# Attention 1 of a graph network: features in two halves, the table in four parts, counts and dense blocks started two blocks earlier

## The chip, the cores and the metric

The kernel runs on one core of a Trainium2 chip. The core has five instruction streams: TensorE (PE, with its weight loads shown as PEld), VectorE (DVE), ScalarE (ACT), GpSimd (POOL) and SyncE (SP, which here only starts transfers). Each engine works through its own list in order; semaphores tie the lists together. The metric is the device time of one execution in microseconds (us), as the median of several runs; lower is better.

## The reference

A pre-norm residual block is applied twice to 6250 nodes of 128 features. The first application is a two-layer graph attention over 200000 edges sorted by destination, the second a graph convolution over the same edges. Cut to what matters here:

```
h  = relu(layernorm(x))
feat = h @ W1;  el = sum(feat*al1);  er = sum(feat*ar1)       # 4 heads of 16
e  = leaky_relu(el[src] + er[dst]);  alpha = softmax of e over the edges of each dst
g  = elu(segment_sum(feat[src] * alpha, dst) + b1)             # attention 1
g2 = the same with W2, one head of 128                         # attention 2
x  = x + g2
x  = x + convolution(relu(layernorm(x)), src, dst, edge attributes)
```

## The kernel before, in words

Nodes are cut into 49 blocks of 128 (`NB`). The program has three large stages: attention 1, attention 2 and the convolution. Only the features and attention 1 are touched by the change.

**Features.** `norm_coefs` computes mean and variance of all 49 blocks on VectorE (`bn_stats`, `bn_aggr`), then one square root on ScalarE, a reciprocal and a bias. Then a loop takes four blocks at a time: ScalarE normalizes (`h`), TensorE transposes, VectorE copies the transposes, TensorE multiplies by the extended weights, ScalarE copies the result into `t1` (64 features and 4 source scores), VectorE copies the destination scores into `er1`. After the loop, two exponentials of the clipped scores complete the 76 columns of `t1`, and one transfer on SP's queue writes `table1` to DRAM (1862 KB). `pq`, `pq3` and `sel1` (factors of the destination side and a steep offset for the dense blocks) come from the same data.

**Attention 1** treats its destination blocks in two ways. The first 31 (`NG = NB - DENSE1`) are attended by gathering. For each block, 34 columns of 128 edges are handled in five groups of 8, 8, 8, 8 and 2 (`GROUPS`, `K = 34`). A group is 8 indirect transfers on GpSimd's queue (`gather`, line 315, table rows into one of six `G` buffers), then `attend`: a one-hot tile, a small product, weights and messages on VectorE, a split into two parts (`halve`: ScalarE casts, VectorE subtracts), and eight accumulating products (line 377). Line 967 is ScalarE's copy that closes a block; every fourth block is finished by `finish1`.

The last 18 blocks (`DENSE1`) are attended densely, two at a time, from a matrix of edge counts: 7 ramps on ScalarE (line 870), a minimum on VectorE (872) and products with the right-hand side `rhs1` (890). `n_dense` = 270 steps cover all of it, 252 of them with 7 ramps each. The count matrices of all 49 blocks are needed (attention 2 reads them as well). They are built in 196 quarter-block steps (`count`: two one-hot tiles on VectorE at line 752, 16 products on TensorE, 4 casts `ca` on ScalarE at 765, one transfer to DRAM), beginning with block 30.

**Order of the work.** The Python loop over the 31 gathered blocks decides what is emitted beside each group. Side work comes first: window searches (`seek_windows`, 25 indirect transfers `wpart_i` on GpSimd and two VectorE operations each), the copies of the edge lists that overlap (`write_runs`, transfers on ScalarE's queue), and `fill_rhs1` (seven fills in blocks 1 and 2). From block `LAG` on, `due` hands out count steps in proportion to the gathers, and from block `LAG_D` on dense steps. `fetch_run` gathers the edge lists of a window on GpSimd (line 710), and `cut_windows` turns them into keys on VectorE (from line 719). A dense pair loads the counts of its blocks on SP's queue, so those must have been written. Within what is emitted, a scheduler of the framework sorts the instructions of each engine ahead of time by its own estimates, so the order in the trace is not quite that of the source. On the engines the order is then fixed.

```python
            if b < LAG - 1:
                for _ in range(2):
                    next(seeking, None)
            if b + 1 < LAG:
                write_runs(b * len(GROUPS) + q, (LAG - 1) * len(GROUPS))
            ...
            due = len(steps) * ((b - LAG) * K + s + n) // ((NG - LAG) * K)
            ...
            due = n_dense * ((b - LAG_D) * K + s + n) // ((NG - LAG_D) * K)
```

Of the kernel before, what the change touches and what calls it, by code (L numbers as in the profile page):

```python
# [30 lines left out]
F32 = mybir.dt.float32  # L31
# [4 lines left out]
AF = mybir.ActivationFunctionType  # L36
OP = mybir.AluOpType
# [5 lines left out]
P = 128  # L43
# [7 lines left out]
WSTEP = 16  # L51
HS = 7
CT, LT = 30, 40
LAG = 5
AHEAD = 4
DENSE1, LAG_D = 18, 7
GP, GK, GSB = 125, 16, 4
SEG = 40
FAR = 1.0e30
# [1 line left out]
SPREAD = 60.0  # L61
SLOPE = 0.2
# [4 lines left out]
def gnn_kernel(ctx: ExitStack, tc: tile.TileContext, x, src, dst, attr4, attr8,  # L67
               W1, al1, ar1, b1, W2, al2, ar2, b2,
               Wl0, Wl1, Ws0, Ws1, Wm1, Wm2, Wtp, Wf0, Wf1, src_t, dst_t, attr4_t, attr8_t, out):
    nc = tc.nc  # L70
    N, D = x.shape
    E = src.shape[0]
    NB = -(-N // P)
    FULL = N // P
    REST = N - FULL * P
    HD = W1.shape[1]
    H1, DH = al1.shape
# [22 lines left out]
    work = ctx.enter_context(tc.tile_pool(name="work", bufs=2))  # L100
# [9 lines left out]
    def small():  # L110
        return ps_sm.tile([P, 512], F32, tag="small", name="small")
# [4 lines left out]
    def bank():  # L116
        return ps_bank.tile([P, 512], F32, tag="small" if ps_bank is ps_sm else "bank", name="bank")
# [40 lines left out]
    pool = one.enter_context(tc.tile_pool(name="att1", bufs=1))  # L158
# [3 lines left out]
    pre = seek.enter_context(tc.tile_pool(name="pre1", bufs=1))  # L162
    xt = pre.tile([P, NB, D], F32, name="xt0")
# [94 lines left out]
    def write_runs(i, n):  # L258

        per = ROWT // WSTEP  # L260
        j, i, n = i * 2 // n, i % (n // 2), n // 2
        ends = [(GP - 1) * i // n, (GP - 1) * (i + 1) // n]
        for p0, p1, m in [(*ends, per)] + [(GP - 1, GP, NROW - (GP - 1) * per)] * (i == n - 1):
            a = raws[j][p0:p1, :]
            nc.scalar.dma_start(
                runs[p0 * per:p0 * per + (p1 - p0) * m, j, :].rearrange("(p r) t -> p r t", r=m),
                bass.AP(tensor=a.tensor, offset=a.offset, ap=[a.ap[0], [WSTEP, m], [1, WCAP]]))
# [18 lines left out]
        nc.vector.tensor_scalar(dstw[:, b, :], raw_dst.pop(b), -float(b * P), None, op0=OP.add)  # L286


    def norm_coefs(pool, b0=0, n=NB):

        mv = pool.tile([P, n, 2], F32, name=f"mv{n}")
        for j in range(n):
            st = work.tile([P, 6], F32, name="bnst")
            nc.vector.bn_stats(st, xt[:, b0 + j, :])
            nc.vector.bn_aggr(mv[:, j, :], st)
        sd = pool.tile([P, n], F32, name=f"sd{n}")
        nc.scalar.activation(sd, mv[:, :, 1], AF.Sqrt, bias=eps)
        scale = pool.tile([P, n], F32, name=f"scale{n}")
        nc.vector.reciprocal(scale, sd)
        bias = pool.tile([P, n], F32, name=f"bias{n}")  # L300
        nc.vector.scalar_tensor_tensor(bias, mv[:, :, 0], -1.0, scale, op0=OP.mult, op1=OP.mult)
        return scale, bias

    def transposed(srcs, rows, evict):

        ps = bank().rearrange("p (j c) -> p j c", j=4)
        for j, s in enumerate(srcs):
            nc.tensor.transpose(ps[:rows, j, :], s, ident)
        t = work.tile([P, 4, P], F32, name="transp")
        evict(t[:rows, :len(srcs), :], ps[:rows, :len(srcs), :])  # L310
        return t
# [30 lines left out]
    def load_low(b):  # L342
        t = aw.tile([P, CAP], BF16, name="oht")
        nc.sync.dma_start(t, dlow[ds(window_start(b), CAP)].partition_broadcast(P))
        return t
# [173 lines left out]
    def rows_of(table, b0, n):  # L519
        return table[b0 * P:(b0 + n) * P, :].rearrange("(b p) f -> p b f", p=P)  # L520
# [20 lines left out]
    table1 = dram.tile([NB * P, R1], F32, name="table1")  # L541
# [21 lines left out]
    er1 = pool.tile([P, NB, H1], F32, name="er1")  # L563

    t1 = pre.tile([P, NB, R1], F32, name="t1")
    scale, bias = norm_coefs(pre)
    for b0 in range(0, NB, 4):
        bs = range(b0, min(b0 + 4, NB))
        hs = []
        for b in bs:  # L570
            h = work.tile([P, D], F32, name="h", bufs=4)
            nc.scalar.activation(h, xt[:, b, :], AF.Relu, bias=bias[:, b:b + 1], scale=scale[:, b:b + 1])
            hs.append(h)
        ht = transposed(hs, D, nc.vector.tensor_copy)
        ps = small()
        w = HD + 2 * H1
        for j in range(len(bs)):
            nc.tensor.matmul(ps[:, j * w:(j + 1) * w], ht[:, j, :], ext1, start=True, stop=True)
        ps = ps[:, :len(bs) * w].rearrange("p (b f) -> p b f", f=w)
        nc.scalar.copy(t1[:, b0:b0 + len(bs), :HD + H1], ps[:, :, :HD + H1])  # L580
        nc.vector.tensor_copy(er1[:, b0:b0 + len(bs), :], ps[:, :, HD + H1:])
    el = pre.tile([P, NB, H1], F32, name="el")
    nc.vector.tensor_scalar(el, t1[:, :, HD:HD + H1], SPREAD, -SPREAD, op0=OP.min, op1=OP.max)
    nc.scalar.activation(t1[:, :, HD + H1:HD + 2 * H1], el, AF.Exp)
    nc.scalar.activation(t1[:, :, HD + 2 * H1:], el, AF.Exp, scale=SLOPE)
    nc.sync.dma_start(rows_of(table1, 0, NB), t1)
    pq = pool.tile([P, NB, 2 * H1], F32, name="pq")
    node_factors(pq, er1, H1)
    split3(pre, pq3, pq, [P, NB, 2 * H1])
# [125 lines left out]
    def cut_windows(c):  # L715
        run = fetched.pop(c)
        si, di = run[:, 0, :], run[:, 1, :]
        hi = cut.tile([P, WCAP], I16, name="hi")
        nc.vector.tensor_scalar(hi, si, 7, None, op0=OP.logical_shift_right)
        key = cut.tile([P, WCAP], F32, name="key")  # L720
        far = cut.tile([P, WCAP], F32, name="far")
        nc.vector.tensor_scalar(key, di, own_w[:, c:c + 1], None, op0=OP.subtract)

        nc.vector.scalar_tensor_tensor(far, key, -1.0, key, op0=OP.add, op1=OP.mult)
        nc.vector.scalar_tensor_tensor(key, hi, float(W), key, op0=OP.mult, op1=OP.add)
        nc.vector.scalar_tensor_tensor(key, far, 1e4, key, op0=OP.mult, op1=OP.add)
        nc.vector.tensor_scalar(hi, si, P - 1, None, op0=OP.bitwise_and)
        lo = far
        nc.vector.tensor_copy(lo, hi)
        m = min(P, NSW - c * P)  # L730
        ps = quad()
        for j, v in enumerate((lo, key)):
            nc.tensor.transpose(ps[:, j, :m], v[:m, :], ident[:m, :m])
        t = cut.tile([P, 2, P], BF16, name="turned", bufs=2)
        nc.scalar.copy(t[:, :, :m], ps[:, :2, :m])
        return t
# [4 lines left out]
    written = set()  # L741
# [239 lines left out]
    for b in range(NG):  # L981
        if b == LAG - 1:
            deque(seeking, 0)
        if b == LAG:
            tables[chunks[0]] = cut_windows(chunks[0])
# [5 lines left out]
        for q, (s, n) in enumerate(GROUPS):  # L991
            step(attending(b, s, n, oht))
            if q == 2 and b + 1 < NG:
                low = load_low(b + 1)
# [5 lines that stand above are left out]
            if b == 1 or b == 2 and q < NB // HS - len(GROUPS):  # L1000
                fill_rhs1(((b - 1) * len(GROUPS) + q) * HS, HS)
            if b == LAG - 1 and q == 3:
                for c in chunks[:2]:
# [30 lines left out]
    xt = ctx.enter_context(tc.tile_pool(name="xt", bufs=1)).tile([P, NB, D], F32, name="xt")  # L1034
# [49 lines left out]
    with tc.tile_pool(name="att2", bufs=1) as pool, tc.tile_pool(name="dense", bufs=2) as dense, \  # L1084
# [8 lines left out]
        def finish2(b0, n):  # L1093
# [10 lines left out]
            nc.vector.tensor_add(xt[:, bs, :], xt[:, bs, :], ps[:, :n * D].rearrange("p (b f) -> p b f", f=D))  # L1104
            yield
            scale, bias = norm_coefs(fin, b0, n)
            t3 = fin.tile([P, 4, D], F32, name="t3")
            for j0 in range(0, n, 2):
# [35 lines left out]
        for b0 in range(0, NB, 2):  # L1144
            n = min(2, NB - b0)
# [10 lines left out]
            for h0 in range(0, NB, HS):  # L1156
# [3 lines left out]
                for h in range(HS):  # L1160
                    nc.scalar.activation(ramp[:, h, :n * P], pe[:, :n * P], AF.Relu,  # L1161
                                         bias=sel2[:, h0 + h, :], scale=STEEP)
                c = ct[:, :n, :, h0:h0 + HS, :].rearrange("p k a h d -> p h (k a) d")
# [12 lines left out]
            for k in range(n):  # L1176
                b = b0 + k
# [5 lines left out]
                                               op0=OP.mult, op1=OP.add)  # L1183
# [102 lines left out]
    with tc.tile_pool(name="conv", bufs=1) as pool, tc.tile_pool(name="gath3", bufs=6) as gath:  # L1286
# [43 lines left out]
        for t in range(0, NT, SB):  # L1330
            n = min(SB, NT - t)
# [8 lines left out]
            for j in range(2 if n > NPR else 1):  # L1340
                c = (t + j * NPR) * P
# [88 lines left out]
```

## Time and profile before

| quantity | value |
|---|---|
| median of 3 runs | 4651.73 us (4643.12 to 4654.26) |
| profiled execution | 4651.0 us, span of its instructions 4649.3 us |
| PE busy | 3221.1 us (69%) |
| DVE busy | 3499.3 us (75%) |
| ACT busy | 2828.8 us (61%) |
| POOL busy | 2785.6 us (60%) |
| first table gather | 133.6 us |
| first run gather | 427.3 us |
| closing copy of gathered block 31 | 1909.3 us |

Busy shares are over the whole span. Times in the trace count from its first instruction. A bracket behind a row says how long the engine was idle before it and what ended the idle time; "issue" is time in which it waited for nothing that the profile shows. ACTq and SPq rows are transfers issued on those engines' queues. A releaser is the last of several semaphores by the profile.

### The profile page before, as it was taken

What the parts mean: (1) busy time and instruction counts of PE and PEld (TensorE: products, weight loads), DVE (VectorE), ACT (ScalarE), POOL (GpSimd) and SP (SyncE); (2) the same over time, 40 slices, a digit from 0 to 9 for tenths busy, and PEclk for the clock granted to TensorE, in tenths of its full rate; (3) what the DMA queues carried; (4) which work ended last, traced back from release to release, by engine and by line L of the source; (5) the groups of instructions that cost most, each with busy time, mean ns of one, the idle gap of its engine ahead of it and who ended that gap; (6) DMA issues with size and microseconds to landing.
All of it is one profiled execution on the core that took longest, in us unless ns stands there. A gap on an engine that the chain in (4) does not pass through costs nothing. (4 is left out here: it accounts for less than half of the span.)

```text
span 4649.3 us, 65503 instructions
## 1 busy us (share of the span) xinstructions
PE 3221.1 (69%) x21547; PEld 2384.9 (51%) x21548; DVE 3499.3 (75%) x5685; ACT 2828.8 (61%) x6834; POOL 2785.6 (60%) x2684
## 2 busy tenths in 40 slices
PE   3023676766667766399997678777777777777777
PEld 3013566656566666388885344444444444444444
DVE  4255777878778878488886787788878777878787
ACT  2022578777878888499996554555555555555554
POOL 0677777666566665100002777777777777777774
PEclk9999766666666666599998676677677777766777
DMA  3344455555555555544442222222222222222221
GB/s 86 69 108 125 139 162 145 157 151 156 144 150 163 164 152 149 184 159 157 160 165 73 57 58 59 58 58 58 58 57 59 58 58 58 58 58 58 58 57 32
DMA packets 348162, 480.88 MB, mean 103 GB/s; under 512 B 190737, under 2 KB 236343, under 8 KB 343830
## 3 DMA queue, kind: packets, MB, share of 16 engines
q1 hardware_dynamic: 199542, 240.46, 16.9%
q0 software_dynamic: 85776, 147.31, 13.4%
q10 hardware_dynamic: 62480, 88.68, 5.6%
q8 instruction: 176, 2.88, 0.3%
q14 instruction: 188, 1.54, 0.1%
HBM read 367.21 MB, written 108.97 MB: 102 GB/s over the span
## 5 line engine op out<-in xcount | busy, mean ns | idle before, releaser
L315 POOL DMA_INDIRECT G<-table,srcc x1563 | 1592.8, 1019 | 1027.5 <-DVE kept L1210 551.4
L315 POOL DMA_INDIRECT G<-table,srcw x1054 | 1121.0, 1064 | 568.2 <-issue 279.0
L1262 PE MATMUL whole<-halves,ohr 128*128 128x512 f32 x1563 | 684.8, 596 | 362.2 <-DVE halves L332 320.1
L870 ACT ACTIVATE ramp<-erb,sel 128x256 bf16<-128x256 f32 x1764 | 759.0, 499 | 11.5 <-DVE up L872 8.0
L1262 PEld LDWEIGHTS whole<-halves,ohr 128*128 128x128 f32 x1563 | 427.5, 288 | 607.6 <-DVE halves L332 392.5
L1243 ACT ACTIVATE g<-G,a 128x128 f32<-128x128 f32 x1563 | 511.0, 395 | 43.5 <-DMA G<-table,srcc 35.0
L1161 ACT ACTIVATE ramp<-small,sel 128x256 bf16<-128x256 f32 (+1 forms) x1225 | 447.6, 625 | 61.1 <-DVE up L1165 26.1
L765 ACT CAST ca<-small 128x392 bf16<-128x392 f32 x784 | 342.1, 481 | 192.1 <-PE small L763 180.4
L890 PE MATMUL up<-rc,up 128*128 128x102 bf16 x3528 | 311.4, 264 | 155.9 <-DVE up L872 154.8
L377 PE MATMUL whole<-halves,ohr 128*128 128x136 f32 x1054 | 250.1, 387 | 224.6 <-DVE halves L332 167.7
L763 PE MATMUL small<-key,lo 128*128 128x98 bf16 x3136 | 318.6, 252 | 116.1 <-ACT ca L765 105.3
L1232 PEld LDWEIGHTS big<-wtp_sb,hid 64*128 64x128 f32 x3126 | 256.7, 239 | 204.7 <-ACT hid L1226 100.7
L890 PEld LDWEIGHTS <-up 128*128 128x128 bf16 x3528 | 265.7, 129 | 183.4 <-DVE up L872 177.4
L332 DVE TENSOR_TENSOR halves<-big,halves 128x1024 fp32r<-128x1024 f32 x196 | 237.4, 1211 | 144.3 <-ACT halves L331 144.3
L872 DVE TENSOR_TENSOR up<-ramp,ctc 128x1792 bf16<-128x1792 bf16 x252 | 273.9, 1087 | 92.7 <-ACT ramp L870 71.3
L1224 PE MATMUL small<-hid,wm_sb 128*128 128x512 f32 x392 | 288.0, 825 | 74.4 <-ACT hid L1222 74.2
L377 PEld LDWEIGHTS whole<-halves,ohr 128*128 128x128 f32 x1054 | 217.3, 292 | 237.1 <-DVE halves L332 172.4
L1232 PE MATMUL big<-wtp_sb,hid 64*128 64x128 f32 x3126 | 307.4, 344 | 26.8 <-ACT hid L1226 26.8
L763 PEld LDWEIGHTS <-lo 128*128 128x128 bf16 x3136 | 247.1, 124 | 145.1 <-issue 126.4
L752 DVE TENSOR_TENSOR lo<-slots,turned 128x2048 bf16<-128x2048 bf16 x196 | 239.0, 1219 | 101.4 <-PE small L763 100.2
L1222 ACT ACTIVATE hid<-small 128x512 f32<-128x512 f32 x196 | 116.8, 596 | 313.7 <-PE small L1220 313.7
L331 ACT CAST halves<-mid 128x1024 fp32r<-128x1024 f32 x196 | 204.1, 1041 | 160.9 <-DVE mid L1251 159.2
(292 smaller groups left out, 6196.7 us busy)
## 6 DMA issues: line engine op xcount, KB each, us to landing
counts<-ca ACTq DMA_DIRECT2D x196, 392.0 KB
ct<-counts SPq DMA_DIRECT2D x196, 392.0 KB
rc<-rhs SPq DMA_DIRECT2D x63, 717.5 KB
oht<-dlow SPq DMA_DIRECT2D x31, 1088.0 KB
ctc<-counts SPq DMA_DIRECT2D x504, 56.0 KB
G<-table,srcc POOLq DMA_INDIRECT x1563
G<-table,srcw POOLq DMA_INDIRECT x1054
a8t<-attr_rows SPq DMA_DIRECT2D x391, 16.0 KB
```

What stands on the lines that cost most here:

```text
L315: nc.gpsimd.indirect_dma_start(out=G[:, c, :], out_offset=None, in_=table, in_offset=bass.IndirectOffsetOnAxis(ap=idx[:, c:c + 1], axis=0))
L377: nc.tensor.matmul(acc, oh[:, c, :], ms[:, c].rearrange("e s f -> e (s f)"), start=start and c == 0, stop=stop and c == n - 1)
L763: nc.tensor.matmul(ps[:, k * NKEY:(k + 1) * NKEY], lo[:, a, :, r], ky[:, a, :, r], start=True, stop=True)
L765: nc.scalar.copy(ca[:, :, i * W:(i + WBANK) * W].rearrange("p h (k d) -> p h k d", d=W), ps[:, :WBANK * NKEY].rearrange("p (k h d) -> p h ...
L870: nc.scalar.activation(ramp[:, i, :n * P], erb[:, h, :n * P], AF.Relu, bias=sel1[:, h0 + i, h:h + 1], scale=STEEP)
L872: nc.vector.tensor_tensor(up[:, :, :n * P].rearrange("p h (a d) -> p h a d", d=QN), ramp[:, :, :n * P].rearrange("p h (a d) -> p h a d", d ...
L890: nc.tensor.matmul(ups[k][:, h], up[:, i, k * P:(k + 1) * P], by_head[:, i, :, h, :], start=h0 + i + h == 0, stop=h0 + i + h == NB + H1 - 2)
L1161: nc.scalar.activation(ramp[:, h, :n * P], pe[:, :n * P], AF.Relu, bias=sel2[:, h0 + h, :], scale=STEEP)
L1224: nc.tensor.matmul(ph[:, :npr * P], wm2_sb, hid1[:, :npr * P], start=True, stop=True)
L1232: nc.tensor.matmul(pw[:, c, :], hid2[half, j * P:(j + 1) * P], wtp_sb[half].rearrange("x p u -> x (p u)"), start=True, stop=True)
L1243: nc.scalar.activation(g0[:, c], G[:, c, :], AF.Copy, scale=a0[:, c, :])
L1262: nc.tensor.matmul(acc, oh[:, c, :], ms[:, c].rearrange("e s h i u -> e (s h i u)"), start=start, stop=stop)
```

## The change

Four edits, all up to the end of attention 1.

1. The statistics of the first 24 blocks (`H0`) are computed ahead of the loop; those of the other 25 are put into the first six turns of the loop, and their coefficients follow in the sixth.
2. The exponentials and the write of `table1` are done in parts of 12, 12, 12 and 13 blocks, the first two after the sixth turn, the others as soon as their blocks are there.
3. `LAG` goes from 5 to 3: counts begin at the gathered block of index 3, window searches are drained at the start of block 2, and `write_runs` cuts its work into 10 pieces over two blocks instead of 20 over four.
4. `LAG_D` goes from 7 to 5, so the dense steps begin at block 5.

The number of count steps and dense steps is the same; they are spread over 28 and 26 blocks instead of 26 and 24.

```diff
-LAG = 5
+LAG = 3
 AHEAD = 4
-DENSE1, LAG_D = 18, 7
+DENSE1, LAG_D = 18, 5
...
-    def norm_coefs(pool, b0=0, n=NB):
-
-        mv = pool.tile([P, n, 2], F32, name=f"mv{n}")
-        for j in range(n):
-            st = work.tile([P, 6], F32, name="bnst")
-            nc.vector.bn_stats(st, xt[:, b0 + j, :])
-            nc.vector.bn_aggr(mv[:, j, :], st)
+    def norm_stats(mv, b):
+        st = work.tile([P, 6], F32, name="bnst")
+        nc.vector.bn_stats(st, xt[:, b, :])
+        nc.vector.bn_aggr(mv, st)
+
+    def norm_coefs(pool, b0, n, mv=None):
+
+        if mv is None:
+            mv = pool.tile([P, n, 2], F32, name=f"mv{n}")
+            for j in range(n):
+                norm_stats(mv[:, j, :], b0 + j)
         sd = pool.tile([P, n], F32, name=f"sd{n}")
...
-    scale, bias = norm_coefs(pre)
+
+    H0 = NB // 8 * 4
+    mv = pre.tile([P, NB - H0, 2], F32, name="mv")
+    el = pre.tile([P, NB, H1], F32, name="el")
+    written = deque((H0 // 2 // 4 * 4, H0, (H0 + NB) // 8 * 4, NB))
+    b_out = 0
+    scale, bias = norm_coefs(pre, 0, H0)
+    co = [(scale[:, j:j + 1], bias[:, j:j + 1]) for j in range(H0)]
     for b0 in range(0, NB, 4):
...
-            nc.scalar.activation(h, xt[:, b, :], AF.Relu, bias=bias[:, b:b + 1], scale=scale[:, b:b + 1])
+            nc.scalar.activation(h, xt[:, b, :], AF.Relu, bias=co[b][1], scale=co[b][0])
             hs.append(h)
+        if b0 < H0:
+            for j in range((NB - H0) * b0 // H0, (NB - H0) * (b0 + 4) // H0):
+                norm_stats(mv[:, j, :], H0 + j)
+        if b0 + 4 == H0:
+            scale, bias = norm_coefs(pre, H0, NB - H0, mv)
+            co += [(scale[:, j:j + 1], bias[:, j:j + 1]) for j in range(NB - H0)]
         ht = transposed(hs, D, nc.vector.tensor_copy)
...
-    el = pre.tile([P, NB, H1], F32, name="el")
-    nc.vector.tensor_scalar(el, t1[:, :, HD:HD + H1], SPREAD, -SPREAD, op0=OP.min, op1=OP.max)
-    nc.scalar.activation(t1[:, :, HD + H1:HD + 2 * H1], el, AF.Exp)
-    nc.scalar.activation(t1[:, :, HD + 2 * H1:], el, AF.Exp, scale=SLOPE)
-    nc.sync.dma_start(rows_of(table1, 0, NB), t1)
+        while written and H0 <= b0 + 4 and written[0] <= b0 + len(bs):
+            c = slice(b_out, written.popleft())
+            nc.vector.tensor_scalar(el[:, c], t1[:, c, HD:HD + H1], SPREAD, -SPREAD, op0=OP.min, op1=OP.max)
+            nc.scalar.activation(t1[:, c, HD + H1:HD + 2 * H1], el[:, c], AF.Exp)
+            nc.scalar.activation(t1[:, c, HD + 2 * H1:], el[:, c], AF.Exp, scale=SLOPE)
+            nc.sync.dma_start(rows_of(table1, c.start, c.stop - c.start), t1[:, c])
+            b_out = c.stop
     pq = pool.tile([P, NB, 2 * H1], F32, name="pq")
```

## The prediction

> **What bounds the kernel now.** I read the stage windows first, because a busy share over 4649 us mixes three stages with different limits. Windows of the whole core (length; PE, PEld, DVE, ACT, POOL busy with instruction counts; granted TensorE clock; DMA share; GB/s):
>
> ```profile
> 133.00:395.00 262.00, 44.71 (x282) 40.77 (x281) 107.11 (x257) 38.17 (x54) 193.80 (x195) 1.00 0.42 101
> 682.00:1840.00 1158.00, 794.97 (x7667) 727.36 (x7667) 911.55 (x1622) 929.78 (x2306) 755.85 (x698) 0.66 0.53 154
> 1840.00:1915.00 75.00, 51.46 (x517) 46.43 (x515) 53.70 (x79) 66.76 (x166) 0.00 (x0) 0.64 0.33 108
> ```
>
> From 133 to 395 us GpSimd (POOL) alone is full: 195 gathers of 0.94 us with 0.3 us of issue after each, about 1.34 us apiece, while ScalarE is at 15% and VectorE at 41%. Counts and dense blocks have not begun. From 682 to 1840 us ScalarE is at 80%, VectorE at 79%, POOL at 65% (and 0.3 us of issue per gather on top). Past the last gather ScalarE rises to 89%. So one regime leaves ScalarE idle and the next leans on it. The same in the windows of the gather's line, L315 (gathers per stretch):
>
> ```profile
> 303.00:395.00 92.00, 70.07 (x69) 1.00 0.62 156
> 700.00:1840.00 1140.00, 723.97 (x668) 0.66 0.53 153
> ```
>
> 1.33 us per gather, or 45 us per block of 34, becomes 1.71 us, or 58 us.
>
> What lengthens a block? The timeline of ScalarE shows each block's closing copy (L967), and the windows of its ramp line, L870, show what was done in between:
>
> ```profile
> 1112.49 0.19 ACT L967 COPY sums<-whole 128x68 f32<-128x68 f32 x1
> 1152.42 0.21 ACT L967 COPY sums<-whole 128x68 f32<-128x68 f32 x1 [4.06 <-PE whole L377]
> 1231.22 0.19 ACT L967 COPY sums<-whole 128x68 f32<-128x68 f32 x1
> 1112.00:1152.00 40.00, 21.40 (x51) 0.66 0.59 175
> 1152.00:1231.00 79.00, 42.13 (x98) 0.66 0.48 137
> ```
>
> Two blocks, each of 34 gathers: 39.9 us with 51 ramps, 78.7 us with 98. Time goes with the counts and dense work, hardly with the gathers.
>
> Ahead of the gathers stands the feature stage. Timeline (start, length, engine, line, work, idle before and its end):
>
> ```profile
> 64.96 0.34 ACT L297 ACTIVATE sd<-mv,eps 128x49 f32<-128x49 f32 x1 [10.37 <-DVE mv L295]
> 66.07 3.96 ACT L572 ACTIVATE h<-xt,bias,scale 128x128 f32<-128x128 f32 x10 [0.78 <-DVE bias L301]
> 108.71 1.28 ACT L584 ACT_TABLE_LOAD   x1 [0.61 <-issue]
> 110.65 0.38 SPq L586 DMA_DIRECT2D table<-t  x1
> 133.60 0.96 POOL L315 DMA_INDIRECT G<-table,srcw  x1 [85.79 <-DMA table<-t]
> 427.28 0.94 POOL L710 DMA_INDIRECT run<-runs,wfirst  x1 [0.30 <-issue]
> 429.81 0.19 DVE L719 TENSOR_SCALAR hi<-run 128x128 int16<-128x128 int16 x1 [21.92 <-DMA run<-runs,wfirst]
> ```
>
> ScalarE waits for all 49 blocks' statistics, the loop runs 66.1 to 108.1 us, the table is issued at 110.65 and the first gather starts 22.9 us later. Counting begins with the first gather of runs at 427.3, and VectorE stood 21.9 us for it.
>
> **What the Trainium skill says.** "Perfetto Trace Analysis", Optimization Strategy: kernels with several regimes may gain by "interleaving those regimes". The windows show two such regimes. "DMA: Bandwidth & Descriptors", Issuing engines are not separate DMA queues: transfers started from any engine share the same 16 DMA engines. The table does land among the run writes of ScalarE's queue, with no gather yet running. "ScalarE: Activation LUTs", What ACT_TABLE_LOAD costs: about 1283 ns plus a drain; the trace has 1.28 us.
>
> **The change, part by part.** The scheduled order of both kernels was compared engine by engine. From attention 2 on, all that ScalarE, GpSimd and VectorE issue keeps its order, so I price nothing there; everything up to the end of attention 1 (1909 us, the last closing copy) moves.
>
> *Statistics in halves.* The 24th block's aggregate was already there at 50.4 us; a mask operation (1.02 us), the reciprocal and the bias follow, so h starts near 52.5 instead of 66.1: 13.6 us earlier. What VectorE did between 51.3 and 65.0 (25 statistics pairs, one-hot tiles) now falls into the loop. A group of four blocks takes 3.41 us there and VectorE is busy 0.85 of it (0.69 copy, 0.16 copy), so six groups offer 15 us for 13.7; in order, between the copies that PE waits for, I charge 3 us. Uncovered it would cost 13.7 and the part would gain nothing.
>
> *The seam.* After the sixth group ScalarE does the exponentials of parts 1 and 2 before the next h: one group's latency (3 us), a table load (1.28) and four short activations (1.1) make 5.4. The later table load at 108.71 goes away. The exponentials of part 3 add 0.7. Loop end: 52.5 + 42.0 + 3 + 5.4 + 0.7 = 103.6 instead of 108.1. The last exponentials queue behind a run write that is now 2500 rows instead of 1200 (issues took 0.8 us, 2.9 and 6.4 when crowded): issue of part 4 near 105.5.
>
> *Table in four parts.* Three parts (36 of 49 blocks) go ahead, so 13/49 of 1862 KB = 494 KB remain. Before, 1862 KB and some 1.2 MB of run writes took 20 us, about 150 GB/s; 494 KB with one to two run writes of 625 KB is 7 to 12 us. I take 9.5, and 0.8 until the gather: first gather at 115.8, so **18 us** earlier. Bounds: 12 (crowded issue) and 26 (no crowding). Three more SP issues of 0.38 us hide, since SP waited from 57 to 110 us.
>
> *Counts at the third block.* In the scheduled order the first run gather stands behind 126 table gathers and 25 window gathers instead of 194 and 25: 68 POOL instructions at 1.35 us, **92 us** earlier, behind a first gather that is itself 18 us earlier, so near 317 us. It needs all 25 window positions (the last now 44 gathers, some 55 us, ahead of it) and the run writes, now ten over two blocks. VectorE reaches it about 10 us after the gather, behind the fills of rhs1 (about 11 us each, interleaved with the gathers of the second and third block), so most of the 21.9 us stand should vanish; I count none of that as gain.
>
> *What it costs.* From 427.3 to 1909.3 are 1482 us, with all 784 count copies and 1764 ramps, and 26 blocks. The same work must still be done, now with 28 blocks. Two more blocks cost at least their ScalarE work: 4.7 us a block (four halvings of 0.65, one of 0.3, closing copies) at 85% use, so 11 us for both. At most their VectorE work: about 19 us a block (one-hot 5.2, node mask 1.4, reduce 1.6, products 5, halves 2.9, finish 2.5) at 79%, 48 us for both. A straight line through the 24 closing intervals from 506 to 1909 us against ScalarE's background work gives 5.6 us per block for attending, with an error of 9: nearer to the low end. I take **35**, as the fills now collide with the first counts. The stage then ends at 317 + 1482 + 35 = 1834 instead of 1909. *Dense at the fifth block* stays two blocks behind the counts, so its first loads wait much as before (SP waited 28.6 us for counts between 330 and 640 us).
>
> Sum: −18 − 92 + 35 = **−75 us**. The profiled execution took 4651.0 us for a span of 4649.3, and the median is 4651.7, so both references give **4576**.
>
> **Rivals.** *A, the forecast* (0.70): 4576, own range 4546 to 4608 from 11 and 48 us for the blocks and 12 to 26 for the table, with some 15 us for a different packing of the same work.
>
> *B, the start chokes* (0.15). Counts, fills and window searches meet on VectorE at 300 us, and the first dense pair needs blocks 30 to 32 counted, 48 copies, with 52 done instead of 56 when it begins. SP's queue stands in order behind such a load, and the next node masks and index windows stand behind it. The block in which dense began took 73.7 us for 70 ramps, 16 more than the line gives. Twice that and a late table: about 4615.
>
> *C, POOL keeps the pace* (0.08). If the gather chain set the block's time, 28 blocks at 57.0 (1482/26) are 1596 us and the stage ends at 1913: 4655, no change. For it: POOL with issue is 83% occupied, and gathers stretch from 0.94 to 1.08 us. Against it: the 39.9 us block.
>
> *D, slower* (0.07). Every G buffer is released by a VectorE product that stands in order behind counts; POOL already waits for such releases (90.4 us behind L362, 42.7 behind L367). If the earlier start makes POOL and VectorE wait for each other, a block costs over 57 us in spite of 7% less background. Break-even is 56.9 us a block, (1482 + 92 + 18)/28; at 58 the stage ends at 1941 and the run takes 4683.
>
> That the change does not do what it says is excluded by the order: four table writes, the run gather at place 126.
>
> **How the numbers follow.** A measurement of this kernel tells about 0.3% (14 us) from no change. A and B are faster; C and D split around zero: faster 0.87, same 0.05, slower 0.08. The range 4540 to 4632 holds A and most of B.
>
> **What would show it.** Right: the first gather near 116 us; the first run gather near 317; hardly any VectorE stand before L738; block intervals of 52 to 54 us; closing copy of the last block near 1834; attention 2 and the convolution as long as before. Wrong: a first gather past 125 us (run writes crowd ScalarE or the landing), intervals still at 57 us with POOL over 90% (C), or long waits of POOL for VectorE products (D).

## The result and the profile after

The changed kernel took 4566.45 us (median of 4 runs, 4562.61 to 4575.01) and the kernel before 4647.42 us on the same chip (4 runs, 4636.58 to 4654.26). The ratio is 0.983, with a 95% interval of 0.9805 to 0.9856: 81 us less, against 75 predicted. The profiled execution took 4562.61 us for a span of 4560.9, which is 88.4 us below the span of before.

One fact has to stand ahead of the experiments. In three of their four groups the kernel before itself took 5583 to 5648 us; in the measurement above and in the last group it took 4647 to 4653 us. Below these are the *long* and the *short* condition. What sets them apart is not known (the recorded chip number of one long group and of the short one is the same), so times are compared within a group only, or between traces of the same condition.

Timeline of the kernel after (start, length, engine, line, work, idle before and its end). Line numbers have moved: what is 301 after is 297 before, and so 583 is 572, 602 is 584, 604 is 586, 319 is 315, 626 is 607, 631 is 612, 729 is 710, 738 is 719 and 986 is 967. 265 is the run write in both, 451 a reduction of VectorE behind the loop. Lines 626 and 631 belong to the window search: its last products on TensorE and the cast of its result.

```profile
52.22 4.34 ACT L583 ACTIVATE h<-xt,bias,scale 128x128 f32<-128x128 f32 x11 [0.67 <-DVE bias L305]
...
71.69 1.28 ACT L602 ACT_TABLE_LOAD   x1
72.99 0.24 ACT L602 ACTIVATE t<-el 128x48 f32<-128x48 f32 x1
...
75.12 0.24 ACT L602 ACTIVATE t<-el 128x48 f32<-128x48 f32 x1 [1.76 <-DVE el L601]
...
96.76 3.23 ACTq L265 DMA_DIRECT2D runs<-raw  x1
100.04 0.25 ACT L602 ACTIVATE t<-el 128x52 f32<-128x52 f32 x1 [3.07 <-DVE far L451]
100.12 9.07 ACTq L265 DMA_DIRECT2D runs<-raw  x1
100.45 0.36 SPq L604 DMA_DIRECT2D table<-t x1
...
107.78 1.79 PE L626 MATMUL small<-ones_b,belowc 125*128 125x1 bf16 x50 [0.18 <-DVE belowc L624]
109.83 0.18 DVE L631 CAST wseg_i<-wseg 128x25 int32<-128x25 f32 x1
110.37 0.96 POOL L319 DMA_INDIRECT G<-table,srcw  x1 [62.21 <-DVE wseg_i L631]
...
312.40 0.94 POOL L729 DMA_INDIRECT run<-runs,wfirst  x1 [1.54 <-DMA runs<-raw]
...
331.41 0.18 DVE L738 TENSOR_SCALAR hi<-run 128x128 int16<-128x128 int16 x1
...
1822.78 0.21 ACT L986 COPY sums<-whole 128x68 f32<-128x68 f32 x1 [0.84 <-PE whole L381]
```

Three differences of these rows account for the time. The first table gather comes at 110.37 instead of 133.60: 23.2 us. From it to the first gather of runs it is now 202.0 us instead of 293.7: another 91.7. From there to the last closing copy it is 1510.4 us instead of 1482.0: 28.4 given back. Together the stage ends 86.5 us earlier. What follows (attention 2 and the convolution) takes 2738.1 us instead of 2740.1.

Stage windows of the kernel after (columns as in the prediction):

```profile
111.00:310.00 199.00, 24.37 (x170) 22.31 (x169) 65.72 (x171) 19.71 (x27) 147.30 (x151) 1.00 0.37 92
600.00:1755.00 1155.00, 793.11 (x7782) 724.59 (x7782) 928.04 (x1656) 936.77 (x2320) 804.43 (x751) 0.67 0.54 157
```

The first window is the stretch in which GpSimd alone is full; between the two first gathers it is now 202 us long, not 294. In the mixed stretch ScalarE is at 81% and VectorE at 80%, hardly more than before (80 and 79), and GpSimd at 70% instead of 65. A mixed block takes 1510.4 / 28 = 53.9 us, where it took 57.0. So the same background work was spread over two more blocks, and each block became shorter.

The waits of GpSimd between 340 and 1740 us (total, times, longest) show that the release of buffers did not become a longer wait:

```profile
POOL G L319 <- issue: 239.0, 784, 0.3
...
POOL G L319 <- DVE w L366: 74.3, 22, 8.7
```

The product that releases a buffer (L362 before, L366 now) had held POOL up 90.4 us; now it is 74.3.

### The profile page after: what moved, and what is told of

Same layout as the page of the kernel before. It is cut to its first block, busy times and chain, and to the rows that moved or that the text cites. A ratio compares the mean times of both kernels' runs of the same rounds, so it can differ in the third digit from the quotient of the medians.

```text
span 4560.9 us, 65476 instructions
## 1 busy us (share of the span) xinstructions
PE 3204.0 (70%) x21547; PEld 2371.8 (52%) x21548; DVE 3493.8 (77%) x5690; ACT 2829.5 (62%) x6841; POOL 2779.0 (61%) x2684
## 3 DMA queue, kind: packets, MB, share of 16 engines
q14 instruction: 188, 1.54, 0.1%
## 5 line engine op out<-in xcount | busy, mean ns | idle before, releaser
L1281 PEld LDWEIGHTS whole<-halves,ohr 128*128 128x128 f32 x1563 | 424.6, 286 | 602.0 <-DVE halves L336 390.5
L381 PE MATMUL whole<-halves,ohr 128*128 128x136 f32 x1054 | 231.9, 372 | 178.4 <-DVE halves L336 127.6
L891 DVE TENSOR_TENSOR up<-ramp,ctc 128x1792 bf16<-128x1792 bf16 x252 | 273.9, 1088 | 85.7 <-ACT ramp L889 72.6
L335 ACT CAST halves<-mid 128x1024 fp32r<-128x1024 f32 x196 | 204.1, 1041 | 161.8 <-DVE mid L1270 160.1
L381 PEld LDWEIGHTS whole<-halves,ohr 128*128 128x128 f32 x1054 | 203.1, 278 | 190.2 <-DVE halves L336 135.6
```

What stands on the lines that cost most here:

```text
L381: nc.tensor.matmul(acc, oh[:, c, :], ms[:, c].rearrange("e s f -> e (s f)"), start=start and c == 0, stop=stop and c == n - 1)
L1281: nc.tensor.matmul(acc, oh[:, c, :], ms[:, c].rearrange("e s h i u -> e (s h i u)"), start=start, stop=stop)
```

## Experiments

The theory, A: background work (counts and dense blocks) sets the pace of a mixed block, so starting it earlier, in a stretch that has room, pays. The rivals: the two parts need each other; the chain of gathers on GpSimd sets the pace (C); the start chokes (B). Further ones came up on the way and belong to the long condition: W (there, waits between engines that a gather causes set the pace of a block), its sharper form S (there, TensorE's signals come late while GpSimd issues long strings of gathers) and P, the rival to S (the gathers' own time sets the pace there, and late signals are a consequence).

### The parts one by one (long condition, one group; before 5647.58 us)

Features alone, counts and dense blocks put back:

```diff
-LAG = 3
+LAG = 5
-DENSE1, LAG_D = 18, 5
+DENSE1, LAG_D = 18, 7
```

> Features in halves and table in parts alone, counts and dense blocks where they were before (LAG 5, LAG_D 7). My theory: all of attention 1 behind the first gather is moved up by as much as the first gather, so first gather near 110 us, first run gather near 404 us, last closing copy near 1886 us, time about 23 us under before. Rival (the table's start is absorbed later, since the mixed regime is bound by its own work): less than 8 us under before.

Counts and dense blocks alone, on the kernel before:

```diff
-LAG = 5
+LAG = 3
-DENSE1, LAG_D = 18, 7
+DENSE1, LAG_D = 18, 5
```

> The kernel before with only LAG 3 and LAG_D 5. My theory: first gather at 133.6 us as before, first run gather near 336 us, about 63 us under before; with the features it adds up to the whole change. Rival (the two parts need each other, because the earlier counts collide with a later feature stage): under 45 us.

The change with its table in one part:

```diff
-    written = deque((H0 // 2 // 4 * 4, H0, (H0 + NB) // 8 * 4, NB))
+    written = deque((NB,))
```

> The changed kernel, but the table is finished and written in one part at the end of the loop; statistics stay in halves. My theory: the 1862 KB land some 20 us after their issue, first gather near 124 us, 12 to 16 us over the changed kernel. Rival (landing is set by the run writes that crowd it, not by the table's size): first gather near 112 us, within 4 us of the changed kernel.

The change with all statistics ahead of the loop, the parts of the table kept:

```diff
...
-    scale, bias = norm_coefs(pre, 0, H0)
+    scale, bias = norm_coefs(pre, 0, NB)
...
-        if b0 < H0:
-            for j in range((NB - H0) * b0 // H0, (NB - H0) * (b0 + 4) // H0):
-                norm_stats(mv[:, j, :], H0 + j)
-        if b0 + 4 == H0:
-            scale, bias = norm_coefs(pre, H0, NB - H0, mv)
```

> The changed kernel, but all 49 blocks' statistics ahead of the loop; the table still in four parts. My theory: h starts near 66 us, the loop is free of statistics, last part issued near 111 us, first gather near 120 us, 8 to 11 us over the changed kernel. Rival (statistics inside the loop cost as much as their start gains): within 3 us of the changed kernel.

| kernel | median us | ratio to before, 95% interval | first gather us |
|---|---|---|---|
| features alone | 5641.94 | 0.9985 (0.9961 to 1.0009) | 109.0 |
| counts and dense alone | 5650.59 | 1.0008 (0.9988 to 1.0028) | 132.2 |
| table in one part | 5631.34 | 0.9977 (0.9957 to 0.9997) | 120.2 |
| statistics ahead | 5639.49 | 0.9998 (0.9973 to 1.0024) | 123.6 |

Theory A's times were not met: expected were 23 us less for the features and 63 us less for counts and dense blocks, measured 6 us less and 3 us more. There was hardly a gain here to take apart. The traces do settle the feature stage, though, since in it the conditions agree: the first gather of the full feature part comes at 109 to 110.5 us in both, and without it at 132 to 134. Without the halves it comes 13 us later than 110.4 (8 to 11 expected), without the parts of the table 10 us later (12 to 16 expected): 23 in sum, as much as the two bring together. To a us or two they neither need nor cover each other.

### The change itself, and more (long condition, one group; before 5583.09 us)

The changed kernel unaltered:

> The changed kernel itself, beside the kernel before on the chip of this job. Theory A (background work of counts and dense blocks sets the pace of attention 1, so starting it 110 us earlier pays): 75 to 88 us below the kernel before. Theory W (on a chip where the kernel before takes about 5650 us, waits between the engines that a gather causes set the pace of a block, and ScalarE and VectorE have room): within 15 us of the kernel before there, as the parts alone were; the last block then closes at 2300 us or later however early counting begins.

Features alone, the same kernel as above:

> The changed kernel with counts put back to five blocks behind and dense blocks to seven; only the feature part is left. Theory A: the first gather is 23 us earlier and everything follows it, 18 to 25 us below the kernel before; the changed kernel then stands 52 to 65 us below this one. Rival (the two parts need each other: without the early table the counts would not have come early): the changed kernel no more than 30 us below this one. Theory W: 0 to 10 us below the kernel before.

Two more gathers in each block, into a buffer that nothing reads:

```diff
+        if s in (0, 16):
+            gather(gath.tile([P, 1, R1], F32, tag="Gx", name="Gx"), table1, srcw[:, b, s:s + 1], 1)
         gather(G, table1, srcw[:, b, s:s + n], n)
```

> The changed kernel with two more one-column gathers in each block, into a buffer that nothing reads (67 more GpSimd instructions of about 1.35 us with their issue, 85 us in all, of which about 8 us lie in the stretch in which GpSimd alone is full). Theory A (ScalarE and VectorE set the pace): 15 to 35 us above the changed kernel, with POOL's wait for released buffers shrinking by the rest. Rival C (the chain of gathers sets the pace): 75 to 95 us above it. Theory W on a slow chip: 0 to 90, by whether a gather costs its time or only its waits.

One block earlier still:

```diff
-LAG = 3
+LAG = 2
-DENSE1, LAG_D = 18, 5
+DENSE1, LAG_D = 18, 4
...
-                for _ in range(2):
+                for _ in range(4):
...
-                write_runs(b * len(GROUPS) + q, (LAG - 1) * len(GROUPS))
+                for i in (2 * q, 2 * q + 1):
+                    write_runs(i, 2 * len(GROUPS))
```

> The changed kernel with counts beginning at the second block of gathers and dense blocks at the fourth, all run writes within the first block. Theory A: one block less runs alone and one more runs mixed: the first gather of runs comes 45 us earlier and the stage loses 14 to 25 us of it, 20 to 31 us below the changed kernel. Rival B (the start chokes: fills, window searches and counts meet on VectorE): no gain or up to 15 us above the changed kernel. Theory W on a slow chip: within 10 us of it.

| kernel | median us | ratio to before, 95% interval |
|---|---|---|
| the change | 5585.42 | 1.0007 (0.9983 to 1.003) |
| features alone | 5570.05 | 0.9981 (0.9952 to 1.001) |
| change, two more gathers a block | 5646.38 | 1.016 (1.0114 to 1.0207) |
| change, one block earlier | 5592.18 | 1.0035 (1.0012 to 1.0058) |

In this condition the change brings nothing, as W had it. The first gather of runs and the last closing copy of the changed kernel here,

```profile
330.12 0.94 POOL L729 DMA_INDIRECT run<-runs,wfirst  x1 [2.13 <-issue]
...
2398.89 0.22 ACT L986 COPY sums<-whole 128x68 f32<-128x68 f32 x1 [0.83 <-PE whole L381]
```

and of the features alone:

```profile
435.88 0.95 POOL L729 DMA_INDIRECT run<-runs,wfirst  x1 [0.30 <-issue]
...
2367.25 0.22 ACT L986 COPY sums<-whole 128x68 f32<-128x68 f32 x1 [0.83 <-PE whole L381]
```

Counting begins 106 us earlier, and the stretch behind it is 2068.8 us instead of 1931.4: the two blocks cost 137 us here, not 28. With the pair of the first group (2076.0 with two blocks more, 1977.0 without) it is 99 us, and the block of the last edit another 37 (2106.2). These are single profiles in a condition whose runs spread by 1%, so a size of about 50 us a block is all that they give; in the short condition it was 14. A mixed block takes 74.3 us with 26 of them, 73.9 with 28 and 72.6 with 29: here a block keeps its time however thinly the background is spread. That has the form of rival C (more blocks do not make a block shorter), in another condition and at another height; that the chain of gathers is the reason is not shown by it. The profiled executions also lie up to 27 us from the medians of their kernels (5565.1 against 5592 for the last edit, 5603.6 against 5585 for the change).

The trace has 62 added gathers, two in each of 31 blocks (the expectation counted 67). At about 1.34 us each with their issue they are 83 us of GpSimd's time, and they cost 61 us against the unaltered change, between what A and C expected. That GpSimd's own work limits the block is only part of it: in the unaltered change it was busy for 48% of the time between 700 and 2300 us, and with 193 us of issue for 60%.

```profile
700.00:2300.00 1600.00, 855.49 (x7676) 764.29 (x7677) 926.28 (x1671) 929.79 (x2286) 760.96 (x736) 0.60 0.40 113
2450.00:3000.00 550.00, 487.90 (x5183) 451.62 (x5183) 468.58 (x850) 490.48 (x1355) 13.38 (x1) 0.98 0.45 158
```

These are windows of the changed kernel in the long condition. In the first, inside attention 1, every engine has much room: ScalarE and VectorE at 58%. The second is attention 2, which gathers nothing, and there all is as fast as in the short condition. From the end of attention 1 to the first gather of the convolution it takes 617 us in the long condition and 619 in the short one. Nearly the whole surplus lies where gathers run: 576 us up to the end of attention 1 and 452 between the first and the last gather of the convolution, of a span that is 1041 us longer. The granted TensorE clock is lower in attention 1 (0.60, where the short condition had 0.67), but in the convolution it is nearly the same (0.69 and 0.71), so the clock alone does not account for the surplus.

The waits in attention 1 (400 to 2350 us) point at TensorE ("remote": a semaphore rose and no instruction that ends near it is recorded):

```profile
ACT ca L784 <- remote: 401.3, 77, 24.3
...
POOL G L319 <- DVE w L366: 372.0, 37, 41.3
```

Here is one of them in the timeline:

```profile
1611.17 1.37 PE L909 MATMUL up<-rc,up 128*128 128x102 bf16 x14 [0.18 <-issue]
...
1623.55 0.94 POOL L319 DMA_INDIRECT G<-table,srcw  x1 [0.30 <-issue]
1624.80 0.95 POOL L319 DMA_INDIRECT G<-table,srcw  x1 [0.30 <-issue]
1626.05 0.94 POOL L319 DMA_INDIRECT G<-table,srcw  x1 [0.30 <-issue]
1631.88 0.87 ACT L784 CAST ca<-small 128x392 bf16<-128x392 f32 x2 [24.31 <-remote]
1631.94 1.22 DVE L771 TENSOR_TENSOR lo<-slots,turned 128x2048 bf16<-128x2048 bf16 x1 [20.83 <-remote]
1632.42 0.18 PEld L752 LDWEIGHTS small<-ident,far 128*128 128x128 f32 x1 [20.10 <-ACT ca L784]
```

TensorE's last recorded product ends at 1612.5. ScalarE and VectorE both wait for its semaphore, and both start 19.3 us later, within 0.1 us of each other; then TensorE goes on. Meanwhile GpSimd issues one gather after the other, until its queue comes to a gather of runs that waits for VectorE. Such late signals can be counted in the traces: ScalarE, VectorE or GpSimd idle for over 2.5 us, waiting for TensorE alone, and started more than 2.5 us after TensorE's last recorded end. Between 400 and 2350 us the change has 55 such waits in the long condition. They fall into 42 stretches of 262 us together, not quite half of the 576 (the expectations below have 46, by a count of nearly the same kind). The short traces, before and after, have none. No engine other than TensorE has more than two. Records are not missing: all these traces hold the same 21547 products. In 86% of the late time a gather was under way or being issued, while gathers take 63% of the stretch.

### Later still, and breaks in the strings (long condition, one group; before 5596.45 us)

The opposite direction:

```diff
-LAG = 3
+LAG = 7
-DENSE1, LAG_D = 18, 5
+DENSE1, LAG_D = 18, 9
```

> The changed kernel with counts at seven blocks behind and dense blocks at nine: the opposite direction from the change. Theory A (first chip: a block alone costs 46 us, a mixed one 14 us more work than its share, so lag is pure loss): about 128 us above the changed kernel, about 45 above the kernel before. Theory S (on a chip where the kernel before takes about 5600 us, TensorE's signals come 3 to 20 us late while GpSimd issues strings of gathers, so that a mixed block costs 74 us however many there are, and one alone about 53): four mixed blocks fewer, 20 to 85 us below the changed kernel and below the kernel before.

Measured: 5624.89 us, ratio 1.0062 (1.0019 to 1.0105), some 28 us slower than before. S expected it faster than before and falls in that form; A expected 45 us above before and has the direction. The 24 mixed blocks took 1889.0 us, 78.7 each: the stretch gets 137 us shorter from 28 to 26 blocks, but only 42 from 26 to 24, so less than 26 blocks no longer swallow the background for nothing. With the first run gather at 266, 330, 436 and 533 us the last block closes at 2372, 2399, 2367 and 2422 us: a flat optimum, on which a shift by two blocks buys nothing. By the medians against before in their own groups the same four stand at +9, +2, −13 and +28 us. (The last of the four is from another group than the others.)

To see whether strings of gathers hold TensorE's signals back, the next two were to cut the strings, in the changed kernel and in the kernel before:

```diff
-        gather(G, table1, srcw[:, b, s:s + n], n)
+        if b >= LAG:
+            for c in range(0, n, 4):
+                gather(G[:, c:c + 4], table1, srcw[:, b, s + c:s + min(n, c + 4)], min(4, n - c))
+                nc.gpsimd.memset(lull, 0.0)
+        else:
+            gather(G, table1, srcw[:, b, s:s + n], n)
...
+    lull = pool.tile([P, 1536], F32, name="lull")
```

> The changed kernel with a GpSimd memset of 128x1536 after every four gathers, from the first block that counts on (9 a block in 28 blocks, 252 in all; 1 to 2 us each as an estimate from the 0.2 us of the 128x128 memset: 9 to 18 us a block on GpSimd). Theory S: the strings are cut, the late signals in attention 1 (46 of them, 260 us between 400 and 2350 us in the changed kernel on such a chip) mostly go, and the time falls by 80 to 260 us below the changed kernel. Rival P (the gathers' own time on GpSimd sets the pace there, the late signals are a consequence): 150 to 350 us above it, as two more gathers a block cost 61 us for 85. On a chip where the kernel before takes about 4650 us there is nothing late to cure, and GpSimd at 55 to 63 us a block costs 50 to 260 us.

> The kernel before with the same memsets after every four gathers, from its sixth block of gathers on. Theory S: late signals go here too, 70 to 240 us below the kernel before; with them gone gathers and counts overlap again, so the changed kernel with memsets stands 40 to 85 us below this one, as the change does on the first chip. Rival P: 130 to 330 us above the kernel before, and no more than 20 us between the two kernels with memsets.

Measured: 5711.56 us (1.0236, 1.0191 to 1.0281) and 5780.49 us (1.0354, 1.0317 to 1.0391). But they did not test what they were for. The row of these memsets in the changed kernel:

```profile
L978 POOL MEMSET lull<- x252: 1368/1378/2449, 3.6 to 890.9; 128x1536 f32 x126
```

They run from 3.6 us on and are through at 891. Nothing in the program ties them to a gather, and the scheduled order has them ahead of gathers that still waited for their table or for a buffer. The kernels therefore show a late start: first run gathers at 480 and 669 us, and stretches of 72.4 and 73.3 us a block behind it. The 69 us between the two say nothing of the change, since the first table gather alone came 65 us later in one (182.8) than in the other (117.8).

### Breaks that hold (short condition; before 4652.90 us)

```diff
-        gather(G, table1, srcw[:, b, s:s + n], n)
+        if b >= LAG:
+            for c in range(0, n, 4):
+                e = min(n, c + 4)
+                for _ in range(4):
+                    nc.gpsimd.memset(G[:, c:e], 0.0)
+                gather(G[:, c:e], table1, srcw[:, b, s + c:s + e], e - c)
+        else:
+            gather(G, table1, srcw[:, b, s:s + n], n)
```

> The changed kernel with four memsets of 128x304 ahead of every four gathers, into the columns that these gathers fill, so that they cannot run ahead; in the scheduled order eight memsets stand before eight gathers, in all 28 blocks that count: no string of gathers is longer than eight, with 3 to 4 us between two (estimate: 0.4 us a memset, from 0.205 us for 128 and 1.37 us for 1536 columns), some 15 us a block or 410 us more on GpSimd. Theory S (on a chip where the kernel before takes about 5600 us, long strings of gathers hold TensorE's signals back): fewer than 15 late signals between 400 and 2350 us where the changed kernel had 46, and a time 30 to 200 us below the changed kernel. Rival P (the gathers' chain paces the block there and the late signals have another cause): 30 or more late signals, and 150 to 400 us above it. On a chip where the kernel before takes about 4650 us: 100 to 250 us above the changed kernel, since GpSimd comes to 60 us a block.

This run fell into the short condition, so it can't answer for late signals: it has none, and neither has the changed kernel there, with strings of over 200 gathers. That alone shows that strings of gathers are not enough to make TensorE late. But it became the one test of rival C in the condition in which the change gains. It took 4711.49 us (4 runs), ratio 1.0126 (1.0101 to 1.0152): 59 us over before, while the change is 81 under its own, so 140 us over the change. The memsets now stand between the gathers (timeline),

```profile
1005.97 0.94 POOL L319 DMA_INDIRECT G<-table,srcw  x1 [0.30 <-issue]
1006.90 2.42 POOL L979 MEMSET G<- 128x304 f32 x8
1009.49 0.95 POOL L319 DMA_INDIRECT G<-table,srcw  x1 [0.17 <-POOL G L979]
```

and the window of the mixed stretch reads

```profile
600.00:1755.00 1155.00, 736.75 (x7078) 672.92 (x7079) 865.27 (x1533) 851.79 (x2107) 944.63 (x1399) 0.65 0.50 144
```

GpSimd's waits in it (600 to 1750 us) are

```profile
POOL G L319 <- issue: 177.0, 566, 2.8
POOL G L319 <- POOL G L979: 24.2, 101, 0.5
```

where the changed kernel has

```profile
POOL G L319 <- issue: 190.6, 625, 0.3
POOL G L319 <- DVE w L366: 74.0, 21, 8.7
```

With the memsets GpSimd is at work or at issue for 944.6 + 177.0 + 24.2 of 1155 us, 99%, and the waits for VectorE's products are gone: here the gather chain does set the pace, and ScalarE falls to 74%. All memsets took 298 us, 10.6 us a block; the stage ended at 1971.1 instead of 1822.8, 148 us later, a block took 59.1 us instead of 53.9. So half of the added time was absorbed, 5.4 us a block. Had C held in the changed kernel, all 298 would have come through. GpSimd is there at 86% with issue, by the rows above; the other 14% are 7.5 us a block, and that is about what is left before a further spreading of the background meets the gathers. The 140 us lie within the 100 to 250 expected, nearer the lower end.

## Why the prediction was right

**The sum.** Predicted were −18 (table), −92 (counts) and +35 (two more blocks), in sum −75 us. Measured on the traces: −23.2, −91.7, +28.4, in sum −86.5, and −88.4 over the span; by the medians −81. Each term had the right sign and place, and the forecast mechanism, A, is the one that the trace shows, but for the wait that ended last ahead of the first gather (under the table below). The table's term was 5.2 us and the blocks' 6.6 us too cautious, 11.8 in all. The 4576 is 13.4 us over the profiled execution and 9.6 over the median of 4566.45. (The own range given for A is narrower than its terms: their ends and the 15 us for packing, added up, give 4529 to 4610, and 4566 lies inside either.)

**Statistics in halves.** h starts at 52.22 (52.5 predicted). From there to the last copy of the sixth group (71.68) it is 19.5 us. Six groups at the pace of 3.41 would have been 20.5, and the same stretch of the kernel before took 21.3. The 3 us charged for statistics among the copies were not there.

**The seam.** The 5.4 us held 3 of a group's latency, which lies inside the 19.5 above, so the two have to be taken together: from the first h to the first h behind the seam (75.40) it is 23.2 us, where 20.5 + 3 + 5.4 = 28.9 were predicted. The table load took 1.28 us, as the Trainium skill has it ("ScalarE: Activation LUTs", What ACT_TABLE_LOAD costs), and the first exponential followed 0.02 us after its end, so of the drain that the page adds nothing shows here. ScalarE then stood 1.76 us for VectorE's clipping of the second part, which the prediction did not have. The loop ended at 96.97, where 103.6 was predicted.

**Table in four parts.** The last exponentials did queue behind a run write: its issue held ScalarE's queue for 3.23 us and ScalarE stood 3.07. (The bracket names VectorE's line 451, but that had ended 0.42 us before, and the activation starts 0.05 us after the issue's end.) The write on SP's queue was issued at 100.45 us (105.5 predicted), and from there to the first gather it took 9.9 us (10.3 predicted). This agreement is luck.

The first gather did not wait for the table last. Its bracket names the window search, not the table, and the semaphore records of the trace say the same: the last part of the table had landed at 107.81, 7.4 us after its issue where 9.5 were taken, and the wait that GpSimd's queue left last, at 109.61, was for TensorE, whose last products of the search (L626) end at 109.57. In the kernel before the search was through at 121.9 and the table landed at 132.78, so this wait lay hidden behind the table, and the prediction did not price it.

The other runs agree. With the features alone of the first group the last part was issued 3.7 us earlier (96.71) and the gather came only 1.35 us earlier, and with the table in one part it is the table again that lands last, at 119.4, 18.5 us after its issue. So against the 18 us the issue gained 5 more than predicted and the landing 2, and a hidden wait took back 1.8; smaller parts would bring nothing more while the search stands there. Why the gather, which does not read the search's result, has to wait for it no run tested; in the source the search's buffers are given back (`seek.close()`) before those of the gathers are laid out. The runs without the halves (13 us) and without the parts (10 us) confirm that the gain has these two sources.

**Counts at the third block.** The count of the instructions ahead was the best step: 92 us predicted, 91.7 measured, the gather of runs at 312.4 (317), after 1.54 us of waiting for a run write. The stand of 21.9 us before line 719 has gone. VectorE got there 19 us after the gather and not 10, without idling just before, so it cost nothing that can be seen.

**What it costs.** The two blocks cost 28.4 us, between the 11 of ScalarE's work and the 48 of VectorE's, below the 35 taken. The block takes 53.9 us, within the 52 to 54 named, and the last block closes at 1822.8 (1834). Dense began with the same two blocks behind the counts: the first ramp came 103 us earlier, without the choke of rival B. Rival C is refuted for this condition by the 53.9 us, where it had 57.0, and by the memsets between gathers; D's break-even of 56.9 us was not reached.

**Where it would have been wrong.** In the long condition the same kernel gains nothing, and there the step "What it costs" fails: two more blocks cost about 100 to 137 us instead of 35. The prediction took the regime from one trace and treated the price of a mixed block as a property of the kernel. Other steps, the feature part and the place of the first run gather (330), hold there too. The advice of the Trainium skill to interleave regimes ("Perfetto Trace Analysis", Optimization Strategy) is borne out in the short condition, 81 us, and not in the long one.

What stays open: why the long condition exists; whether TensorE is really late there or its last instructions run longer than they are recorded, and what part the lower granted clock has in it; whether gathers cause it, since the run that was to tell fell into the short condition; and where the half of the surplus that the counted signals don't hold goes. How the 81 us divide over the parts was not timed in the short condition. It rests on the positions in the two traces, one execution each, and on the feature stages of the first group. Whether one block earlier pays in the short condition was not tried there.

## What to carry to other kernels

If one stretch leaves two engines idle and the next leans on them, price a shift as two terms: how many instructions stand ahead of the moved start (that can be counted, and was right to 1 us), and what an added block costs in the mixed stretch (this decides the sign, and can only be bounded). The second term depends on what the other engines do in that moment, and it changed from 28 to about 100 us or more with the condition of the machine, so measure a change that rests on overlap more than once and in more than one session. When the wait that ended last gets shorter, look for the one just behind it: here the window search held the first gather 1.8 us beyond its table. An instruction that is meant to separate others needs a data dependence on them; the 252 memsets without one were scheduled elsewhere, those that wrote into the gathers' columns stayed.

## What the runs showed of the hardware

- TensorE's signals came 2.5 to 20.2 us after its last recorded end, in 42 stretches of attention 1, in the long condition alone. The median durations of the instructions themselves were the same (a gather 0.94 us in the short and 0.95 in the long condition, a product of line 909 0.28 us in both), and attention 2, without gathers, was not slower.
- The issue of a run write on ScalarE's queue took between 0.75 and 10.9 us (12 of them in the changed kernel, median 0.82). ScalarE itself stood 3.07 us behind the one that took 3.23.
- From its issue to its landing a table write of 494 KB took 7.4 us in the changed kernel; one of 1862 KB took 22.1 us in the kernel before and 18.5 us in the changed kernel with its table in one part, all with run writes beside them.
- A memset of 128x1536 on GpSimd took 1.38 us, eight of 128x304 back to back 2.42 us.
